# A two-layer gated cross-attention kernel: in the first network's second step, the first inner row's maximum and rounding are put behind the gate of the step's second block

## The chip, the cores and the metric

The kernel runs on one core of a Trainium2 chip. The metric is device time in microseconds (us) of one execution. Three timed executions of the kernel before gave 729.78, 729.82 and 726.80 us; the median is 729.78 us. One more execution was recorded by the hardware profiler.

## The reference, cut to what matters

The input x has 8 x 256 = 2048 rows of 512 values. Four stages change it one after the other, each added to x with a gate factor tanh(g):

1. a long convolution of the context with 32 heads, multiplied with the normalised x,
2. a first feed-forward network with weights rounded to -1, 0 or 1 and activations rounded to 8 bits,
3. a masked attention over the context,
4. a second feed-forward network with signs for weights.

The change lies in stage 2. For each row of x:

```python
def _activation_quant(x):
    scale = 127.0 / jnp.clip(jnp.max(jnp.abs(x), axis=-1, keepdims=True), 1e-05, None)
    xq = jnp.clip(jnp.round(x * scale), -128.0, 127.0) / scale
...
h = jax.nn.silu(_bitlinear(x, w1)) * _bitlinear(x, w2)      # 512 -> 1408
return _bitlinear(h, w3)                                    # 1408 -> 512
```

`_bitlinear` first rounds its input row by row. So the inner row h, 1408 values wide, needs its absolute maximum over the whole row before it can be scaled, rounded to int8 and sent through the third weight.

## The kernel before, in words

The 2048 rows are cut into 16 tiles of 128 rows, one row for each partition. Stage 2 is a loop of 17 steps (`for t in range(NT + 1)`), software-pipelined by hand: the order of the statements is the order in which each engine gets its instructions, since the program is under a manual schedule. Each engine works through its own list in that order; waits between engines are semaphores which the tile framework puts in. In step t the kernel

- makes the inner row of tile t, `hh` (128 x 1408), in three blocks of columns, by `up_block` (L854 to L872) at columns 0, 512 and 1024. This document calls them blocks A, B and C; A and B are 512 wide, C is 384 wide. A block is four matmuls on TensorE into `pa` and four into `pb` (L860), a SiLU of `pa` on ScalarE into `sl` (L868), and the gate on VectorE, `hh = pb * f * sl` (L869). `pa` and `pb` come from a ring of four PSUM buffers, so that the `pa` of a block takes the buffer of the `pa` two blocks earlier and waits for that block's SiLU, and its `pb` waits for that block's gate. Block A of step 2 waits in this way for block B of step 1;
- takes the maximum of the inner row of tile t-1 on VectorE by `row_max(h_[t - 1], "h")` (the maximum at L518, then two small instructions at L520 and L522 that end in the scale `sc`), and rounds this row on ScalarE into `i8h` (L1019), GpSimd clips it to bf16 into `qh` (L1037), and a transposing DMA on the SyncE queue brings it to the layout that TensorE needs, `hqT` (L1039);
- multiplies the inner row of tile t-2 by the third weight on TensorE (`down0`, L877, eleven matmuls into `po`); tile 0 is done at the end of step 2;
- prepares tile t+2: `front_norm` on ScalarE (L201), `front_max` on VectorE (L518 again, on 512 columns), `front_int` on ScalarE (L537), `front_turn` on GpSimd and the SyncE queue (L541 to L545), which ends in the transposed `xqT`;
- in steps 1 to 3 also finishes stage 1 for the tiles with odd numbers: `odd_back` transposes a tile back on TensorE (`tr_back`, L424), ScalarE scales it out of PSUM (`back`, L989), GpSimd adds it to x (L990). There are two PSUM buffers for these transposes, so that the third `tr_back`, the first of step 2, waits for the first `back`;
- in step 1 also makes the reciprocal deviations of four tiles by `ln_finish` (three small instructions on VectorE, then fourteen on GpSimd).

From step 2 on, the maximum of the previous inner row stands ahead of block A's gate, and its rounding ahead of block B's SiLU. In step 1 of the kernel before it is:

- VectorE: gate of block A, the three instructions of `ln_finish`, maximum of inner row 0, maximum of the front row 3, gate of block B, gate of block C;
- ScalarE: SiLU of block A, rounding of inner row 0, SiLU of block B, rounding of the front row 3 (`i8x`), `back`, SiLU of block C, `back`, normalisation of the front row 4, and then step 2's SiLU of block A.

The lines of before which the change touches are L1013 to L1019, between `up_block(*x0[t], hh, 0)` and `up_block(*x0[t], hh, 512)`:

```python
if t == 1:

    ln_finish(*FINISH[0])
    inv, sc = row_max(h_[0], "h")
if 1 <= t:
    q = p1.tile([P, FF0], I8, tag="i8h", name="i8h")
    nc.scalar.activation(q, h_.pop(t - 1), AF.Copy, scale=sc)
```

Of the kernel before, what the change touches and what calls it, by code (L numbers as in the profile page):

```python
# [12 lines left out]
I8 = mybir.dt.int8  # L13
# [3 lines left out]
AF = mybir.ActivationFunctionType  # L17
# [4 lines left out]
P = 128  # L22
# [11 lines left out]
FF0, FF1 = 1408, 2048  # L34
# [8 lines left out]
def flamingo_gated_kernel(  # L43
# [15 lines left out]
    nc = tc.nc  # L59

    def pool(stack, name, bufs, **kw):
        return stack.enter_context(tc.tile_pool(name=name, bufs=bufs, **kw))
# [146 lines left out]
    def load_table(func):  # L209

        nc.scalar.activation(junk1, ln_eps, func)
# [15 lines left out]
    def residual(t, po, factor):  # L227
        nc.vector.scalar_tensor_tensor(
            xs[:, t, :], po, factor, xs[:, t, :], op0=ALU.mult, op1=ALU.add
        )  # L230
# [284 lines left out]
    def row_max(v, tag):  # L515

        am = small.tile([P, 1], F32, tag="am" + tag, name="am")
        nc.vector.tensor_reduce(am, v, AX.X, ALU.max, apply_absolute_value=True)  # L518
        inv = small.tile([P, 1], F32, tag="inv" + tag, name="inv")
        nc.vector.tensor_scalar(inv, am, Q_EPS, 1.0 / 127.0, ALU.max, ALU.mult)  # L520
        sc = small.tile([P, 1], F32, tag="sc" + tag, name="sc")
        nc.vector.reciprocal(sc, inv)  # L522
        return inv, sc

    def front_norm(k):
        xn0[k] = pf.tile([P, L], F32, tag="xn", name="xn2")
        if k < GRP:
            ln_apply_act(xn0[k], order0[k], *firsts[k // 2], k % 2)
        else:
            ln_apply_act(xn0[k], order0[k], *st0[k // GRP][1:], k % GRP)  # L530
# [305 lines left out]
    p1 = pool(s_mid, "p2one", 1, side="right", reuse_waits="tile")  # L836
# [17 lines left out]
    def up_block(xqT, f1, hh, f0):  # L854
        fw = min(512, FF0 - f0)
        pa = ps_mm.tile([P, 512], F32, tag="mm", name="pa")
        pb = ps_mm.tile([P, 512], F32, tag="mm", name="pb")
        for i, pp in ((0, pa), (1, pb)):
            for c in range(NL):
                nc.tensor.matmul(  # L860
                    pp[:, :fw],
                    xqT[:, c, :],
                    w0q[i][:, c, f0 : f0 + fw],
                    start=(c == 0),
                    stop=(c == NL - 1),
                )
        sl = p2.tile([P, 512], F32, tag="sl", name="sl")
        nc.scalar.activation(sl[:, :fw], pa[:, :fw], AF.Silu, scale=f1[:, 0:1])  # L868
        nc.vector.scalar_tensor_tensor(  # L869
            hh[:, f0 : f0 + fw], pb[:, :fw], f1[:, 1:2], sl[:, :fw],  # L870
            op0=ALU.mult, op1=ALU.mult,
        )  # L872
# [11 lines left out]
    scale = 1.0 / math.sqrt(L)  # L884
# [34 lines left out]
    def batch_gate(neg):  # L919

        valid = small.tile([P, 1], F32, tag="valid", name="valid")
        nc.vector.tensor_reduce(valid, neg, AX.X, ALU.max)
        gv = small.tile([P, 1], F32, tag="gv", name="gv")
        nc.vector.tensor_scalar(gv, valid, 0.0, gate_x[1], ALU.is_equal, ALU.mult)
        return gv

    def normalised3(t, by_pool=False):
        xn = p3.tile([P, L], F32, tag="xn", name="xn3")
        rstd, nmr = st3[t // GRP][1:]
        if by_pool:  # L930
            c = slice(t % GRP, t % GRP + 1)
            nc.gpsimd.tensor_scalar(xn, xs[:, t, :], rstd[:, c], nmr[:, c], ALU.mult, ALU.add)
        else:
            ln_apply_act(xn, t, rstd, nmr, t % GRP)
        return xn
# [12 lines left out]
    def scores(xT, cT):  # L948
        ps = ps_mm.tile([P, 512], F32, tag="mm", name="ps")
        for c in range(NL):  # L950
            nc.tensor.matmul(  # L951
                ps[:, :S], xT[:, c, :], cT[:, c, :], start=(c == 0), stop=(c == NL - 1)
            )
        return ps
# [30 lines left out]
    def odd_back(t):  # L985

        back_transpose(t)
        o = pc.tile([P, L], F32, tag="xn", name="back")
        nc.scalar.activation(o, trs.pop(t), AF.Copy, scale=gate_x[0])  # L989
        return lambda: nc.gpsimd.tensor_tensor(xs[:, t, :], xs[:, t, :], o, ALU.add)  # L990

    h_, d_, hq_ = {}, {}, {}

    BACK = {1: [0, 1], 2: [2, 3, 4], 3: [5, 6, 7]}
    signs, sums, made = [], [], 0
    for t in range(NT + 1):
        new = t + 2 < NT
        if t < NT:
            hh = p2.tile([P, FF0], F32, tag="hh", name="hh")
        if new and t > 0:  # L1000
            front_norm(t + 2)
        if t > 1:
            inv, sc = row_max(h_[t - 1], "h")
        if t == NT:
            xn_[2] = normalised3(2)
            load_table(AF.Exp)
            gates3 = {0: batch_gate(negs[0])}
            ps_ = {k: scores(xT_.pop(k), keys[0]) for k in range(2)}
        if t < NT:
            up_block(*x0[t], hh, 0)  # L1010
        if t == 0:
            front_norm(t + 2)
        if t == 1:  # L1013

            ln_finish(*FINISH[0])
            inv, sc = row_max(h_[0], "h")
        if 1 <= t:
            q = p1.tile([P, FF0], I8, tag="i8h", name="i8h")
            nc.scalar.activation(q, h_.pop(t - 1), AF.Copy, scale=sc)  # L1019
        if t == NT - 2:  # L1020
            xn_ = {k: normalised3(k) for k in range(2)}
        if t >= 3:
            residual(order0[t - 3], *d_.pop(t - 3))
        back = BACK.get(t, [])
        if len(back) == 3:
            sums.append(odd_back(odds[back[0]]))
        if new:
            front_max(t + 2)
        if t < NT:
            up_block(*x0[t], hh, 512)  # L1030
        if t == NT - 1:
            xT_ = {k: x_transposed(xn_.pop(k), True) for k in range(2)}
        if new:
            front_int(t + 2)
        if 1 <= t:
            b = p2.tile([P, FF0], BF16, tag="qh", name="qh0")
            nc.gpsimd.tensor_scalar(b, q, 127.0, -128.0, ALU.min, ALU.max)  # L1037
            bT = p_hq.tile([P, NF0, P], BF16, tag="hqT", name="hqT")
            nc.sync.dma_start_transpose(out=bT, in_=b)  # L1039
            f3 = small.tile([P, 1], F32, tag="f3", name="f3")  # L1040
            nc.gpsimd.tensor_scalar(f3, inv, gw0, None, ALU.mult)
            hq_[t - 1] = (bT, f3)
        if t == NT - 2:
            keys, values = {0: load_keys(0)}, {0: load_values(0)}
        if new:
            front_turn(t + 2)
        for add in sums:
            add()
        sums = []
        if back:  # L1050
            sums.append(odd_back(odds[back[-2]]))
        if t > 2:
            hqT, f3 = hq_.pop(t - 2)
            d_[t - 2] = (down0(hqT), f3)
        if t in FINISH and t > 0:
            ln_finish(*FINISH[t])

        for k in STATS3.get(t, ()):
            ln_moments_of(st3, natural, k, "3")
        if t > 0:  # L1060
            for k in STATS0.get(t, ()):
                ln_moments_of(st0, order0, k, "0")
        if t < NT:
            up_block(*x0.pop(t), hh, 1024)
            h_[t] = hh
        if t == 2:

            hqT, f3 = hq_.pop(0)
            d_[0] = (down0(hqT), f3)
        if back:  # L1070
            sums.append(odd_back(odds[back[-1]]))
        for add in sums:
            add()
        sums = []
        if t == 0:
            clip_by_act(2, 3)
        if t == 3:
            s_conv.close()
            wp1 = pool(ctx, "w1", 1, reuse_waits="tile")
            w1q = [wp1.tile([P, NL, FF1], F32R, name=f"w1_{i + 1}") for i in range(2)]  # L1080
            p_st = pool(s_att, "w1st", 3, reuse_waits="tile")
        if t == NT - 3:
            p3 = pool(s_att, "p3", 2, reuse_waits="tile")
        if t < NT:
            for make in signs:
                make()
            signs = []
        if 3 <= t < NT:
            signs = [w1_signs(made + k) for k in range(2)]
            made += 2  # L1090
        if t == NT - 2:
            bytes_ = {b: load_mask(b) for b in range(2)}
        if t == NT - 1:
            negs = {0: key_mask(bytes_.pop(0))}
        if t == NT:
            negs[1] = key_mask(bytes_.pop(1))
# [105 lines left out]
    for t in range(NT + 2):  # L1202
# [19 lines left out]
        if t == NT:  # L1222
            xn4, q, back = front(1)
# [60 lines left out]
        if t == NT - 3:  # L1284
            q = front_int4(xn4, back)
# [15 lines left out]
    with ExitStack() as ph:  # L1301
# [11 lines left out]
        p1 = pool(ph, "p4one", 1, reuse_waits="tile")  # L1313
# [186 lines left out]
```

## Time and profile before

| | before |
|---|---|
| median of 3 timed executions | 729.78 us (726.80 to 729.82) |
| the profiled execution: its time | 731.69 us |
| the profiled execution: span from first to last instruction | 729.8 us |
| TensorE busy | 713.4 us of the span |
| VectorE busy | 598.6 us |
| ScalarE busy | 371.6 us |
| GpSimd busy | 260.8 us |
| mean granted TensorE clock | 0.992 of full speed |

Engines in the profile are PE (TensorE's matmuls), PEld (its weight loads, which overlap the matmuls), DVE (VectorE), ACT (ScalarE), POOL (GpSimd) and SPq (the queue of SyncE that issues DMAs). A row of the timeline has the start in us from the span's start, the time in us, the engine, the line, the operation with output and input, and in brackets the idle time ahead of it with what ended it. Stage 1 fills the span's first 181 us, the loop of stage 2 goes from 181 us to about 315 us, and the two later stages take the rest. Step 1 of the loop begins at 185.9 us, step 2 at 194.7 us.

### The profile page before, as it was taken

The numbers are of one execution on the slowest core, as the hardware profiler recorded it, in microseconds if no ns is written. First come the engines' busy times: TensorE is split into PE (matmuls) and PEld (weight loads), VectorE is DVE, ScalarE is ACT, GpSimd is POOL, SyncE is SP. The second block draws the span as 40 slices with busy tenths as digits, with TensorE's granted clock in tenths as the row PEclk, the third lists the DMA queues.
The fourth block names the chain that finished last, engine by engine and source line by source line (L and its number), as shares of the span: only waits on it lengthen the run. The fifth ranks groups of instructions, "written<-read, shape, count | busy, mean of one in ns | idle before, by whom it ended". The sixth has DMA issues, their size and how long they took to land.

```text
span 729.8 us, 10128 instructions
## 1 busy us (share of the span) xinstructions
PE 713.4 (98%) x3200; PEld 532.0 (73%) x3200; DVE 598.6 (82%) x1224; ACT 371.6 (51%) x669; POOL 260.8 (36%) x366
## 2 busy tenths in 40 slices
PE   7999999999899999899999999999999999999997
PEld 6777777777454444556668888888888888888885
DVE  5799888999788888777868988988888988777965
ACT  5577887879777777657652222322222332212322
POOL 4788997989874535245300020000200002000000
PEclk8999999999999999999999999999999999999999
DMA  5775676831136565797704455544553444554443
GB/s 196 238 240 159 188 266 202 281 85 32 35 84 139 141 142 141 159 279 219 225 27 96 103 110 110 115 96 110 113 115 83 110 103 104 118 110 91 102 90 86
DMA packets 149970, 99.36 MB, mean 136 GB/s; under 512 B 83806, under 2 KB 127838, under 8 KB 149918
## 3 DMA queue, kind: packets, MB, share of 16 engines
q1 hardware_dynamic: 149608, 98.38, 51.2%
q0 software_dynamic: 256, 0.26, 1.0%
q8 instruction: 25, 0.41, 0.2%
q14 instruction: 27, 0.22, 0.1%
q10 hardware_dynamic: 54, 0.08, 0.1%
HBM read 75.58 MB, written 5.03 MB: 110 GB/s over the span
## 4 chain that ended last, share of the span: by engine, by line
PE 82%; DVE 5%; DMA 4%; POOL 3%; issue 3%; ACT 2%; SPq 0%; DVEq 0%; ACTq 0%; POOLq 0%
PE y L349 17%; PE po L1375 16%; PE pb L1181 15%; PE pa L1181 15%; PE po L877 4%; PE pa L860 4%; PE pb L860 4%; PE po L980 2%; PE ps L951 2%; DMA w1st<-in_L_w3t 2%; DMA hqT<-qh 1%; POOL kv L326 1%; PE tr L416 1%; POOL prod L394 1%; DMA sT<-d 1%
## 5 line engine op out<-in xcount | busy, mean ns | idle before, releaser
L349 PE MATMUL y<-kv,toep 128*128 128x288 f32 x640 | 161.1, 409 | 0.9 <-DVE prod L384 0.7
L349 PEld LDWEIGHTS y<-kv,toep 128*128 128x128 f32 x640 | 120.1, 191 | 33.5 <-ACT qx L313 0.9
L1189 ACT ACTIVATE sl<-pa,wmean 128x512 f32<-128x512 f32 x64 | 44.0, 688 | 195.1 <-PE pa L1181 195.1
L1375 PE MATMUL po<-w,lo 128*128 128x512 f32 x256 | 99.9, 390 | 0.0
L1375 PE MATMUL po<-w,hi 128*128 128x512 f32 x256 | 99.6, 389 | 0.0
L181 POOL TENSOR_TENSOR nwt<-rstd 128x4 f32<-128x4 f32 x33 | 6.6, 199 | 235.1 <-DVE rstd L176 233.2
L326 POOL TENSOR_TENSOR kv<-cx 128x1024 f32<-128x1024 f32 x32 | 60.6, 1895 | 24.2 <-ACT cx L313 24.0
L1181 PE MATMUL pa<-w,hi 128*128 128x512 f32 x256 | 69.2, 392 | 0.0
L1181 PE MATMUL pb<-w,hi 128*128 128x512 f32 x256 | 68.6, 390 | 0.1
L1181 PE MATMUL pa<-w,lo 128*128 128x512 f32 x256 | 68.5, 389 | 0.0
L1181 PE MATMUL pb<-w,lo 128*128 128x512 f32 x256 | 68.4, 389 | 0.0
L860 PEld LDWEIGHTS <-xqT 128*128 128x128 bf16 x384 | 37.9, 99 | 41.2 <-issue 3.1
L394 POOL TENSOR_TENSOR prod<-prod 128x1024 f32<-128x1024 f32 x28 | 66.3, 2368 | 0.0
L1155 ACT CAST hi<-v 128x512 fp32r<-128x512 f32 x64 | 39.2, 622 | 47.9 <-DVE v L1365 47.9
L1193 DVE SCALAR_TENSOR_TENSOR hh<-pb,wmean,sl 128x512 f32<-128x512 f32 x64 | 47.8, 747 | 14.7 <-PE pb L1181 14.5
L1375 PEld LDWEIGHTS po<-w,lo 128*128 128x128 f32 x256 | 48.0, 188 | 10.9 <-DVE lo L1160 1.0
L1181 PEld LDWEIGHTS pa<-w,hi 128*128 128x128 f32 x256 | 47.8, 188 | 10.8 <-ACT hi L1155 0.6
L1181 PEld LDWEIGHTS pb<-w,hi 128*128 128x128 f32 x256 | 48.0, 188 | 10.5 <-DVE hh L1193 0.6
L1181 PEld LDWEIGHTS pa<-w,lo 128*128 128x128 f32 x256 | 48.1, 188 | 10.0
L1375 PEld LDWEIGHTS po<-w,hi 128*128 128x128 f32 x256 | 48.1, 188 | 9.9
L1181 PEld LDWEIGHTS pb<-w,lo 128*128 128x128 f32 x256 | 48.0, 188 | 10.0
L371 DVE TENSOR_TENSOR prod<-y,qx 128x512 f32<-128x512 f32 x64 | 43.8, 684 | 8.6 <-ACT y L359 4.4
(163 smaller groups left out, 1345.3 us busy)
## 6 DMA issues: line engine op xcount, KB each, us to landing
sT<-d SPq DMA_DIRECT2D x64, 256.0 KB
toep<-ssm_skip SPq DMA_DIRECT2D x31, 256.0 KB
ch<-in_ctx_heads SPq DMA_DIRECT2D x32, 128.0 KB
w1a<-in_L_w1t SPq DMA_DIRECT2D x8, 512.0 KB
w1a<-in_L_w2t SPq DMA_DIRECT2D x8, 512.0 KB
w1st<-in_L_w1t SPq DMA_DIRECT2D x16, 256.0 KB
w1st<-in_L_w2t SPq DMA_DIRECT2D x16, 256.0 KB
cT<-in_ctx_t SPq DMA_DIRECT2D x8, 512.0 KB
```

What stands on the lines that cost most here:

```text
L326: nc.gpsimd.tensor_tensor(kv[:, :, 0 : ND * HD].rearrange("p a (i d) -> p a i d", d=ND), cx[:, :, 0:HD].unsqueeze(3).to_broadcast([P, NL * ...
L349: nc.tensor.matmul(y[:, k, :, W0 : W0 + NPAIR], toeps[h][:, d * P : (d + 1) * P], kvs[h][:, mi * B : (mi + 1) * B, :].rearrange("p b n -> ...
L371: nc.vector.tensor_tensor(prod[:, 0, r, :, :], yv[:, :, W0 : W0 + ND * HD].rearrange("p a (i d) -> p a i d", d=ND), view(q, [HX, n], [1, H ...
L394: nc.gpsimd.tensor_tensor(flat[0], flat[0], flat[1], ALU.add)
L860: nc.tensor.matmul(pp[:, :fw], xqT[:, c, :], w0q[i][:, c, f0 : f0 + fw], start=(c == 0), stop=(c == NL - 1),)
L877: nc.tensor.matmul(po, hqT[:, c, :], w0q[2][:, c, :], start=(c == 0), stop=(c == NF0 - 1))
L951: nc.tensor.matmul(ps[:, :S], xT[:, c, :], cT[:, c, :], start=(c == 0), stop=(c == NL - 1))
L1155: nc.scalar.copy(hi, v)
L1181: nc.tensor.matmul(pp, xT[k][:, c, :], w1q[i][:, c, f0 : f0 + 512], start=(c == 0 and k == 0), stop=(c == NL - 1 and k == 1),)
L1189: nc.scalar.activation(sl, pa, AF.Silu, scale=wmean1[:, 0:1])
L1193: nc.vector.scalar_tensor_tensor(hh, pb, wmean1[:, 1:2], sl, op0=ALU.mult, op1=ALU.mult)
L1375: nc.tensor.matmul(po, hT[b][k][:, c, :], w1q[2][:, b * NL + c, :], start=(b == 0 and c == 0 and k == 0), stop=(b == NB - 1 and c == NL - ...
```

## The change

It leaves `ln_finish` where it is, puts the rounding into a small function, and moves the maximum and the rounding of inner row 0 from ahead of block B to behind it in step 1 alone. All other steps issue what they issued before.

```diff
+    def hidden_int(k, sc):
+        q = p1.tile([P, FF0], I8, tag="i8h", name="i8h")
+        nc.scalar.activation(q, h_.pop(k), AF.Copy, scale=sc)
+        return q
...
         if t == 1:
-
             ln_finish(*FINISH[0])
-            inv, sc = row_max(h_[0], "h")
-        if 1 <= t:
-            q = p1.tile([P, FF0], I8, tag="i8h", name="i8h")
-            nc.scalar.activation(q, h_.pop(t - 1), AF.Copy, scale=sc)
+        if t > 1:
+            q = hidden_int(t - 1, sc)
...
         if t < NT:
             up_block(*x0[t], hh, 512)
+        if t == 1:
+
+            inv, sc = row_max(h_[0], "h")
+            q = hidden_int(0, sc)
```

The order of instructions in step 1 becomes:

- VectorE: gate of block A, the three of `ln_finish`, maximum of the front row 3, gate of block B, maximum of inner row 0, gate of block C;
- ScalarE: SiLU of block A, SiLU of block B, rounding of inner row 0, rounding of the front row 3, `back`, SiLU of block C, and so on as before.

The lists of TensorE, GpSimd and the SyncE queue keep their order. No instruction is added or taken away.

## The prediction

> **What bounds the kernel now.** I read the page first. TensorE is busy for 98% of the span, so only TensorE's idle time, or its slow time, can be won. Then I asked who TensorE's matmuls waited for between 186 and 203 us, around the change:
>
> ```profile
> PE 713.4 (98%) x3200; PEld 532.0 (73%) x3200; DVE 598.6 (82%) x1224; ACT 371.6 (51%) x669; POOL 260.8 (36%) x366
> ```
> ```profile
> PE pa L860 <- ACT sl L868: 3.0, 1, 3.0
> ```
>
> One wait of 3.0 us, and it is the place that the change touches. The chain of work that ended last, followed through 186 to 203 us, leaves TensorE just here (start, us, what):
>
> ```profile
> 189.35 0.75 DVE hh L869
> ...
> 190.69 1.53 DVE am L518
> ...
> 192.60 0.59 DVE am L518
> ...
> 194.01 0.68 ACT sl L868
> ...
> 194.73 1.16 PE pa L860 x4
> ```
>
> The gate of block 1A, the maximum of inner row 0, then the SiLU of block 1B, which frees the PSUM buffer that `pa` of block 2A takes. The timelines of ScalarE, TensorE and its weight loads show why:
>
> ```profile
> 188.64 0.67 ACT L868 ACTIVATE sl<-pa,f 128x512 f32<-128x512 f32 x1
> 192.64 1.47 ACT L1019 ACTIVATE i8h<-hh,sc 128x1408 int8<-128x1408 f32 x1 [3.32 <-DVE sc L522]
> 194.01 0.67 ACT L868 ACTIVATE sl<-pa,f 128x512 f32<-128x512 f32 x1
> 194.58 0.71 ACT L537 ACTIVATE i8x<-xn,sc 128x512 int8<-128x512 f32 x1
> 195.19 0.67 ACT L989 ACTIVATE back<-tr_back,gates 128x512 f32<-128x512 f32 x1
> 195.76 0.57 ACT L868 ACTIVATE sl<-pa,f 128x384 f32<-128x384 f32 x1
> ```
> ```profile
> 191.08 0.60 PE L424 MATMUL tr_back<-ident,qT 128*128 128x128 f32 x4
> 194.73 1.16 PE L860 MATMUL pa<-w,xqT 128*128 128x512 bf16 x4 [3.05 <-ACT sl L868]
> 195.68 1.91 PE L860 MATMUL pb<-w,xqT 128*128 128x512 bf16 x4
> 197.39 1.06 PE L424 MATMUL tr_back<-ident,qT 128*128 128x128 f32 x4
> 198.24 1.36 PE L860 MATMUL pa<-w,xqT 128*128 128x512 bf16 x4
> ```
> ```profile
> 192.75 0.10 PEld L860 LDWEIGHTS <-xqT 128*128 128x128 bf16 x1 [1.31 <-DMA xqT<-qx]
> ```
>
> ScalarE stands for 3.32 us at the rounding of inner row 0, with the ready SiLU of 1B behind it, and TensorE stands for 3.05 us. Two more things are to be seen. The weight load shows that block 2A could not have begun before 192.75 us: its transposed input came then. And behind the stall four groups take from 194.73 to 199.43 us, 4.70 us, where groups of these sizes take 0.86 + 0.86 + 0.43 + 0.87 = 3.02 us at full clock: 1.68 us more. The table of windows says why (busy us of PE, PEld, DVE, ACT and POOL, then the granted clock):
>
> ```profile
> 192.00:195.40 3.40, 0.67 (x4) 0.41 (x5) 2.12 (x7) 2.76 (x4) 2.58 (x11) 1.00 0.04 8
> 195.40:198.90 3.50, 3.50 (x12) 1.85 (x11) 2.49 (x5) 2.79 (x5) 3.23 (x6) 0.51 0.49 93
> ```
>
> The clock was halved for 3.4 us behind the stretch in which TensorE did 0.67 us of work. So the place costs 3.05 + 1.68 = 4.73 us, of which 1.2 us (191.68 to 192.85, the weight load included) is the input's and stays. From 202 to 277 us TensorE is busy without a gap and the clock is 1.00: what is won or lost at the first third-weight product (`po`, at 202.03 us) is passed on whole.
>
> **The change, step by step.** Times are those of the profiled execution; an engine's instructions follow each other by their start-to-start distances in its rows.
>
> VectorE. The third instruction of `ln_finish` starts at 190.52, the next at 190.60. In place of inner row 0's maximum the front row's comes first. Its three instructions take 0.97 us (192.52 to about 193.49 in before). Then the gate of 1B at 191.57: its SiLU is long done, and it takes 0.66 us to the next start, 0.75 alone (ends 192.32). Then inner row 0's maximum, 192.23, with 2.04 us from its start to the rounding's start on ScalarE, as before (190.60 to 192.64). So the rounding starts at 194.27, not 192.64: 0.97 + 0.66 = 1.63 us later.
>
> ScalarE. The SiLU of 1B is ahead of the rounding now: 188.64 + 0.57 = 189.21, ended by 189.9 (its matmuls ended at 188.65). This takes 0.57 us out from behind the rounding. All that is queued behind it (the front row's rounding, `back`, SiLU of 1C, `back`, normalisation, SiLU of 2A) is therefore 1.63 - 0.57 = 1.06 us later than before: `i8x` at 195.64, the first `back` at 196.25 (ends 196.92), SiLU of 1C at 196.82 (ends 197.39), SiLU of 2A at 198.56 (ends 199.23).
>
> TensorE. `pa` of 2A starts at 192.85, as soon as its input is there, and not at 194.73. `pb` at 193.71 (the gate of 1B ended at 192.32), ended 194.57. Next in its list is the third `tr_back`, which needs the PSUM buffer of the first: `back` ends at 196.92, so it starts at 197.07. This is a new stall of 2.50 us, in place of the old one of 3.05. Then `pa` of 2B at 197.50 (SiLU of 1C ended 197.39), `pb` at 198.36 (gate of 1C: 197.43 to 198.05), `tr_back` at 199.22, `pa` of 2C at 199.65. `pb` of 2C needs the gate of 2A. On VectorE this stands behind the gate of 1C and the maximum of inner row 1, all 1.06 us later than before: 198.98 + 1.06 = 200.04, ended 200.79. So `pb` of 2C at 200.83, and `po` at 201.48, against 202.03: 0.55 us earlier, if the clock stays full.
>
> What else is moved. The rounded row 0 is ready at 195.74; GpSimd's clip goes from 194.76 to 195.78, the transposing DMA behind it on SyncE's queue from 196.15 to 197.17, and the front row's DMA behind that from 197.71 to 198.73, with GpSimd's additions. The nearest row for the landing, the last such transpose, is 3.50 us from issue (308.75) to TensorE's start (312.25): 200.67, 0.81 us ahead of `po`. The front row's is wanted at 204.3. Both are at no cost; the cover is TensorE's own work up to 201.48, and without it each us of delay is a us. The next inner row's rounding (200.13, not 199.13) and its transpose (issued 203.03, so landed by about 206.5) are wanted at 208.6. No queue is blocked that TensorE reads from later.
>
> **The unknown: the clock behind the new stall.** In the place of one gap of 3.05 us there are two, 1.2 and 2.50 us, with 1.72 us of matmuls between. The Trainium skill, "TensorE: Matmul & The Clock Gate", section "Why this matters for your kernels", asks for no gaps over about 3 us between bursts; by that rule the new gaps leave the clock alone and the sum is -0.55. The page's Part 1 has free-running windows of 3413 ns, which fits the 3.4 us here. The rows speak for a stricter gate. The clock falls after a window with 0.67 us of work in 3.40. At the start of the span it falls too, and stays low, with far more:
>
> ```profile
> 4.33:7.74 3.41, 2.15 (x17) 1.74 (x15) 2.78 (x10) 1.52 (x3) 2.09 (x2) 1.00 0.96 342
> 7.74:11.15 3.41, 2.12 (x9) 1.73 (x10) 3.24 (x13) 2.93 (x6) 0.99 (x2) 0.50 0.70 261
> ```
>
> 63% busy by matmul spans was not enough. The emptiest window I found that kept the clock, 308.1 to 311.5 us, has 2.53 us, 74%. With the boundary of before (195.4) the new windows hold 1.72 us (50%) and 1.8 us (53%); with any other, one holds less, down to 0.91 us (27%). So I expect one cold window. Its cost depends on its place: from 195.4 to 198.9 it slows `tr_back` and most of `pa` 2B, but the wait for the gate of 2A takes some of it back, and `po` comes at 201.86, 0.17 us earlier than before. From 198.0 to 201.4 it slows 2B's `pb` and `tr_back`, and `po` comes at 202.5, 0.5 later; the worst single place I find is 0.6 later. Ends: -0.55 (no cold window) and +1.5 (two, below); below -0.55 is excluded, as the chain over VectorE to the gate of 2A does not run on TensorE's clock. I take +0.2, the middle of one cold window's -0.2 to +0.6: 731.69 + 0.2 = 731.9 us for a profiled execution. The median of the runs lies 1.91 us under the profiled execution (729.78 to 731.69), so 730.0 us.
>
> **The rivals.**
>
> - *The stall moves and the clock stays full.* -0.55: 729.2 us. For it speaks the skill's 3 us, against it the start of the span. Chance 0.25.
> - *The stall is gone.* All but the input's 1.2 us is won: 4.73 - 1.17 = 3.56 us, 726.2 us. It needs ScalarE to come to `back` in time; but the rounding cannot start before 194.27, and `back` and the SiLU of 1C are behind it. Chance 0.04.
> - *Slower: the clock stays low for two windows.* Place: 195.4 to 202.3 us. It decides if the window from 195.4 to 198.9, 53% busy at half clock, is too empty to raise the clock again; at the span's start one with 62% was. Then `pa` 2B ends at 199.63, `pb` 201.34, `tr_back` 202.19, 2C at about 203.55, and `po` is 1.5 us later than before: 731.3 us. Chance 0.18.
> - *The transposed row 0 is late.* At 299.02 a transpose took 5.36 us beside weight loads; from 197.17 that ends at 202.53, +0.5: 730.3 us. Between 196 and 200 us the queue moves only these two transposes, so it is unlikely: 0.05.
>
> **How the numbers follow.** Forecast 0.48, at 730.0 (729.6 to 730.4 by itself). The executions of one and the same kernel are 726.80 to 729.82, a spread of 3.0 us whose cause no row shows and which is larger than all cases but one. So the range is 726.8 (the lowest run; a little above the case of no stall) to 732.0 (two cold windows and half a window's loss more). 0.5% is 3.65 us, about what a measurement of this kernel can tell from no change: under 726.1 is faster, over 733.4 slower. Only the vanished stall comes near the first, only two cold windows together with an unlucky spread near the second: 0.05 and 0.05, same 0.90.
>
> **What would show it.** In the changed kernel's timelines: the SiLU of 1B near 189.2 and the rounding near 194.3 with about 4.4 us idle ahead of it; TensorE's 3.05 us wait replaced by two, the second of about 2.5 us at a `tr_back` that waits for `back`; the third-weight product between 201.5 and 203.6; in the table of windows the clock at 0.5 for one stretch between 193 and 202. It is wrong if the rounding starts before 194, if the second gap is missing, or if the times differ by more than 2 us in either direction with the loop's later steps no longer contiguous.

## The result, and the profile after

The changed kernel takes 729.37 us (median of 12 executions, 727.5 to 732.8), the kernel before 729.80 us (12 executions, 726.8 to 732.12). The ratio of after to before on record is 1.0006 with a 95% interval of 0.9991 to 1.0021; the quotient of the two medians, 0.9994, lies inside it. A second comparison gave 1.0012 (0.9998 to 1.0027). No difference that can be measured.

The profiled execution of after took 732.8 us, the longest of the twelve; its span is 731.0 us, and TensorE is busy for 715.5 us of it. The rows below answer to those shown of before. First the waits of TensorE between 186 and 206 us:

```profile
PE tr_back L424 <- ACT back L989: 2.3, 1, 2.3
PE pa L860 <- DMA xqT<-qx: 1.3, 1, 1.3
```

One wait of 3.0 us has become two, of 1.3 and 2.3 us, with other names: `pa` of block 2A waits for its input, and the third transpose waits for `back`. The timelines of ScalarE and TensorE:

```profile
189.16 1.25 ACT L868 ACTIVATE sl<-pa,f 128x512 f32<-128x512 f32 x2
194.85 1.47 ACT L996 ACTIVATE i8h<-hh,sc 128x1408 int8<-128x1408 f32 x1 [4.44 <-DVE sc L522]
...
196.84 0.67 ACT L989 ACTIVATE back<-tr_back,gates 128x512 f32<-128x512 f32 x1
197.41 0.57 ACT L868 ACTIVATE sl<-pa,f 128x384 f32<-128x384 f32 x1
```
```profile
193.33 1.04 PE L860 MATMUL pa<-w,xqT 128*128 128x512 bf16 x4 [1.25 <-DMA xqT<-qx]
...
197.56 0.66 PE L424 MATMUL tr_back<-ident,qT 128*128 128x128 f32 x4 [2.33 <-ACT back L989]
198.05 1.45 PE L860 MATMUL pa<-w,xqT 128*128 128x512 bf16 x4
199.29 1.91 PE L860 MATMUL pb<-w,xqT 128*128 128x512 bf16 x4
...
203.19 2.54 PE L877 MATMUL po<-w,hqT 128*128 128x512 bf16 x11
```

The two SiLUs (x2) now run one behind the other at 189.16, but the rounding begins only at 194.85, and `back` and the SiLU of 1C behind it. `pa` and `pb` of block 2B are slow again. The windows (busy us of PE, PEld, DVE, ACT, POOL, then the clock):

```profile
195.10:198.50 3.40, 1.07 (x8) 0.70 (x8) 0.49 (x1) 3.40 (x6) 2.05 (x4) 1.00 0.00 0
198.50:201.90 3.40, 3.40 (x12) 1.77 (x11) 3.30 (x6) 2.47 (x4) 3.11 (x4) 0.50 0.76 145
```

The clock is halved for one window of 3.4 us here too, about 3 us later in the span than in before.

Step 1 starts at slightly different times in each execution, so from here on places are counted from the start of block 1A's gate on VectorE (189.35 us in before, 189.87 in after). The **measure** is the time from there to the first matmul of the first third-weight product: 202.03 - 189.35 = 12.68 us in before, 203.19 - 189.87 = 13.32 us in after.

### The profile page after: what moved, and what is told of

The parts are those of the page before. It is cut to its first block, busy times and chain, and to the rows that moved or that the text cites. A ratio compares the mean times of both kernels' runs of the same rounds, so it can differ in the third digit from the quotient of the medians.

```text
span 731.0 us, 10128 instructions
## 1 busy us (share of the span) xinstructions
PE 715.5 (98%) x3200; PEld 534.2 (73%) x3200; DVE 598.6 (82%) x1224; ACT 371.5 (51%) x669; POOL 260.3 (36%) x366
## 4 chain that ended last, share of the span: by engine, by line
PE 89%; DMA 4%; DVE 3%; issue 2%; POOL 1%; ACT 1%; SPq 0%; DVEq 0%; ACTq 0%; POOLq 0%
PE y L349 22%; PE po L1382 16%; PE pb L1188 15%; PE pa L1188 15%; PE po L877 4%; PE pa L860 4%; PE pb L860 4%; PE po L980 3%; PE ps L951 3%; DMA hqT<-qh 1%; PE tr L416 1%; PE tr_back L424 1%; DMA w1st<-in_L_w3t 1%; PE tr L940 1%; DMA sT<-d 1%
```

## The experiments

The theory is the prediction's: the change takes away the wait for the SiLU of 1B, but makes the rounding 1.63 us later on VectorE, and what stands behind the rounding on ScalarE 1.06 us later; so TensorE stalls again, and the clock can fall behind either stall. The rivals: another bound holds the stretch anyway (the transposed input, GpSimd); or the clock is no part of it.

| kernel | measure, us | stretch at half clock in it | ratio to before, 95% interval |
|---|---|---|---|
| before; once more | 12.68; 12.70 | yes; yes | |
| after; once more | 13.32; 12.15 | yes; no | 1.0006 (0.9991 to 1.0021); 1.0012 (0.9998 to 1.0027) |
| before, gap filled | 11.10 | no | 0.9971 (0.9957 to 0.9985) |
| after, gap filled | 12.15 | no | 0.9986 (0.9966 to 1.0005) |
| ScalarE's half alone | 10.52 | no | 0.9976 (0.9961 to 0.9991) |
| after, `back` ahead of the rounding | 11.58 | no | 0.9996 (0.9983 to 1.0009) |
| after, inner row ahead of front row | 11.20 | no | 0.9995 (0.9981 to 1.0009) |

One microsecond is 0.14%, about the half-width of these intervals; so the measure of the profiled executions carries the argument, and the ratios only say whether it is contradicted.

**ScalarE's half alone.** The maximum stays where it was, the rounding is moved:

```diff
         if t == 1:
             ln_finish(*FINISH[0])
+            inv, sc = row_max(h_[0], "h")
...
         if t == 1:
-
-            inv, sc = row_max(h_[0], "h")
             q = hidden_int(0, sc)
```

> One half of the change alone: on ScalarE the rounding of inner row 0 stands behind the SiLU of block 1B, on VectorE its maximum stays ahead of the gate of 1B. The measure is the time from the gate of block 1A (VectorE) to the first third-weight product (TensorE): 12.68 us before, 13.32 us after. Theory: the old stall comes from ScalarE's order alone, and what spoils the change is VectorE's half, which makes the rounding 1.63 us later. Then here the rounding starts as early as before (3.3 us behind the gate of 1A, not 5.0), everything behind it on ScalarE is 0.6 us earlier than before, TensorE's gaps are the input's 1.2 us and several of under 0.6 us, the clock is not halved, and the measure is 10.6 us: about 2.1 us less time than before, 0.3%. Rival (the transposed input or the transposed inner row is the bound): the measure stays at 12.0 us or more and the time is within 0.7 us of before.

Measured: 12.68 becomes 10.52 us, and the time is 0.9976 of before (0.9961 to 0.9991), about 1.8 us less. ScalarE and TensorE in this kernel, whose gate of 1A is at 187.67 us:

```profile
190.97 1.47 ACT L996 ACTIVATE i8h<-hh,sc 128x1408 int8<-128x1408 f32 x1 [2.75 <-DVE sc L522]
...
192.96 0.67 ACT L989 ACTIVATE back<-tr_back,gates 128x512 f32<-128x512 f32 x1
```
```profile
191.09 1.04 PE L860 MATMUL pa<-w,xqT 128*128 128x512 bf16 x4 [1.09 <-DMA xqT<-qx]
192.63 1.02 PE L860 MATMUL pb<-w,xqT 128*128 128x512 bf16 x4 [0.50 <-DVE hh L869]
193.68 0.65 PE L424 MATMUL tr_back<-ident,qT 128*128 128x128 f32 x4
```

The rounding stands 3.3 us behind the gate of 1A, as in before, and `back` frees the transpose's buffer just as TensorE comes to it. The stall of before was ScalarE's order alone; VectorE's half is what spoils the change. Its interval lies below 1, so it is faster than before, and it only touches those of after (0.9991 to 1.0021, and 0.9998 to 1.0027) at its upper end: this half of the change beats both kernels (after by way of before; the two were not timed side by side). VectorE's half alone was not tried: with the rounding still ahead of the SiLU of 1B and its maximum behind the gate of 1B, each of the two engines would wait for the other for ever.

**Each stall by its name.** In after, the first `back` is issued ahead of the rounding:

```diff
         if t == 1:
-
+            sums.append(odd_back(odds[back[-2]]))
             inv, sc = row_max(h_[0], "h")
             q = hidden_int(0, sc)
...
-        if back:
+        if back and t > 1:
             sums.append(odd_back(odds[back[-2]]))
```

> The changed kernel, with the first scaling of a transposed tile out of PSUM (back) issued ahead of the rounding of inner row 0 on ScalarE. Theory: the new stall at the third transpose is this back's place in ScalarE's list. Here that transpose follows block 2A at once, and the wait goes on to the next thing behind the rounding, the SiLU of 1C, for which block 2B waits about 1.9 us. Measure from the gate of 1A to the first third-weight product: 11.6 us at full clock, up to 12.4 with a cold window (after: 13.32). Rival (the third transpose waits for something else, for instance for GpSimd's addition): the gap ahead of the transpose stays over 2 us and the measure stays at 13 us.

The measure is 11.58. TensorE's rows:

```profile
191.86 0.60 PE L424 MATMUL tr_back<-ident,qT 128*128 128x128 f32 x4
194.24 1.02 PE L860 MATMUL pa<-w,xqT 128*128 128x512 bf16 x4 [1.78 <-ACT sl L868]
```

The transpose no longer waits; the wait goes to the next thing behind the rounding, the SiLU of 1C. The third transpose was held by nothing else.

**What VectorE puts ahead of the rounding.** In after, the front row's maximum goes behind inner row 0's:

```diff
-        if new:
+        if new and t != 1:
             front_max(t + 2)
...
             inv, sc = row_max(h_[0], "h")
             q = hidden_int(0, sc)
+            front_max(t + 2)
```

> The changed kernel, with the maximum of the front row 3 behind that of inner row 0 on VectorE. It takes one of the two things away (0.97 of the 1.63 us) that the change put ahead of the rounding on VectorE. Theory: the rounding starts 4.0 us behind the gate of 1A (after: 4.98), all that stands behind it on ScalarE is as much earlier, the wait of the third transpose shrinks from 2.3 to 1.4 us, and the measure from the gate of 1A to the first third-weight product is 11.2 us at full clock (after: 13.32 with a cold window, 12.15 with its gap filled). Rival (the front row's rounding, now waiting for its maximum, holds ScalarE instead): the transpose's gap stays over 2 us and the measure at 12.1 us or more.

The rounding stands 193.43 - 189.44 = 3.99 us behind the gate of 1A (4.98 in after), the wait ahead of the transpose is 1.35 us, the measure 11.20:

```profile
196.14 0.66 PE L424 MATMUL tr_back<-ident,qT 128*128 128x128 f32 x4 [1.35 <-ACT back L989]
```

So of the 1.69 us by which after starts the rounding later than before (4.98 against 3.29), the front row's maximum is 0.99, and the other 0.70 stay with the gate of 1B still ahead. The ratio, 0.9995 (0.9981 to 1.0009), shows no gain: the profiled execution's 1.5 us less than before would be 0.9980, just outside the interval. That execution kept its clock; an estimate further down suggests that some of the timed ones did not.

**The clock.** The stalls are filled with matmuls whose result is not used; all other instructions and their order stay:

```diff
+        if t == 2:
+            fill = ps_o.tile([P, L], F32, tag="o", name="fill")
+            for _ in range(9):
+                nc.tensor.matmul(fill, w0q[0][:, 0, :P], w0q[0][:, 0, :L], start=True, stop=True)
```

in after behind `up_block(*x0[t], hh, 0)`, and in before the same with twelve matmuls ahead of it.

> The changed kernel with nine extra matmuls of 128x512 (about 1.9 us, their result is not used) put into TensorE's new gap between block 2A and the third transpose. Theory of the clock: the halved clock behind the gap costs the changed kernel about 1.2 us, and a gap that is filled leaves the clock at 1.00; the measure from the gate of 1A to the first third-weight product falls from 13.32 to about 12.1 us and the time by about 1.2 us. Rival (the clock falls anyway, or its loss is hidden by the waits for VectorE): the measure stays at 13.0 us or more.

> The kernel before with twelve extra matmuls of 128x512 (about 2.6 us, their result is not used) put into TensorE's old gap of 3.05 us ahead of block 2A. Theory: with the clock kept at 1.00 the kernel before reaches the first third-weight product 1.6 us earlier: measure from the gate of 1A 11.1 us, not 12.68, and then the order of before is a whole 1.0 us better than the changed order with its gap filled: the change by itself makes the path longer, and only the clock's loss, which comes in both, hides it. Rival (the clock makes no difference to the end of this stretch): measure 12.6 us, and the two filled kernels equal.

Measured: 12.15 and 11.10 us. TensorE in before with its gap filled (gate of 1A at 186.93):

```profile
189.10 2.75 PE L1012 MATMUL fill<-w 128*128 128x512 bf16 x12
192.34 1.02 PE L860 MATMUL pa<-w,xqT 128*128 128x512 bf16 x4 [0.48 <-ACT sl L868]
193.20 1.03 PE L860 MATMUL pb<-w,xqT 128*128 128x512 bf16 x4
194.06 0.60 PE L424 MATMUL tr_back<-ident,qT 128*128 128x128 f32 x4
```

`pa` of 2A still waits for the same SiLU and starts no earlier (192.34 - 186.93 = 5.41 us behind the gate of 1A, 194.73 - 189.35 = 5.38 in before), but what follows takes 1.03 and 0.60 us, not 1.91 and 1.06. So before's stall costs 12.68 - 11.10 = 1.6 us by the clock alone. And with the clock held, the changed order is 12.15 - 11.10 = 1.05 us longer than the order of before. The change has a loss of its own, the 1.06 us forecast on ScalarE; what hides it is that before pays for a cold clock more often than after does, as the executions below show.

After and before once more, for the clock:

> The changed kernel once more, for its clock. Theory: its stall is the same to 0.1 us in each execution (2.3 us at the third transpose, 1.25 us at block 2A), and whether the clock is halved behind it depends on how the clock's windows fall: measure from the gate of 1A to the first third-weight product 12.1 us without a cold window, up to 13.4 us with one. Rival: the measure is 13.3 us again with the clock at 1.00, and the clock is no part of it.

> The kernel before once more, for its clock. Theory: stall of 3.05 us again, measure from the gate of 1A to the first third-weight product 11.1 us without a cold window, 12.7 us or a little more with one. Rival: 12.7 us with the clock at 1.00.

After again (gate of 1A at 187.76): the same two waits, no cold window, measure 12.15.

```profile
191.19 1.04 PE L860 MATMUL pa<-w,xqT 128*128 128x512 bf16 x4 [1.10 <-DMA xqT<-qx]
195.41 0.65 PE L424 MATMUL tr_back<-ident,qT 128*128 128x128 f32 x4 [2.32 <-ACT back L989]
195.90 1.03 PE L860 MATMUL pa<-w,xqT 128*128 128x512 bf16 x4
```

Before again: 3.06 us of stall, half clock from 196.1 to 199.5 us, measure 12.70. In each profile the recorded changes of the clock lie whole steps of 3.413 us apart (in before, those at 7.75, 195.48 and 727.96 us are 55.0 and 156.0 steps from one another), so the windows can be placed also where nothing changes. Those of both, after first (cut at steps of 3.4 us back from where its clock falls at the end of the span), then before:

```profile
190.10:193.50 3.40, 1.90 (x8) 0.70 (x8) 2.50 (x4) 0.80 (x1) 2.17 (x11) 1.00 0.15 28
193.50:196.90 3.40, 1.49 (x9) 0.97 (x10) 1.00 (x2) 3.40 (x6) 2.38 (x4) 1.00 0.01 3
```
```profile
192.70:196.10 3.40, 1.07 (x5) 0.58 (x6) 1.82 (x6) 3.17 (x5) 2.68 (x9) 1.00 0.00 0
196.10:199.50 3.40, 3.40 (x12) 1.75 (x11) 2.73 (x5) 2.47 (x6) 3.13 (x6) 0.50 0.61 115
```

In after's second profile the idle time was split over two windows, which kept 56% and 44% of work and the full clock. In before's second profile 1.07 us (31%) were left in one, and the clock fell. In after's first profile it was 1.07 us too.

How often this happens can be estimated from the mean granted clock, which is on record for the timed executions too. In the ten profiles it is 0.999 or 1.0 without a cold window, 0.998 with one at this place, 0.994 to 0.995 with two near the span's start, and 0.992 to 0.993 with both. Sorted by this (0.997 put with 0.998, 0.996 with 0.995), 77 of 117 executions of before had a cold window here, 11 of 34 of after, 2 of 21 of before with its gap filled, and 6 of 22 of the kernel with the inner row first. With the measures above that makes 11.10 + 0.66 x 1.6 = 12.2 us for before and 12.15 + 0.32 x 1.2 = 12.5 us for after, a difference of about 0.4 us or 0.05%, which both intervals of after allow.

**A version that removes all of it.** The maximum of inner row 0 was kept early, everything that frees a buffer of TensorE was put ahead of the rounding, and the first third-weight product behind block 3A (edits cut to their core):

```diff
         if t == 1:
             ln_finish(*FINISH[0])
+            inv, sc = row_max(h_[0], "h")
...
         if t == 1:
+            sums.append(odd_back(odds[back[-2]]))
+            up_block(*x0.pop(t), hh, 1024)
+            h_[t] = hh
+            sums.append(odd_back(odds[back[-1]]))
             q = hidden_int(0, sc)
+            front_max(t + 2)
...
+        if t == 1:
+            front_turn(t + 2)
         if 1 <= t:
             b = p2.tile([P, FF0], BF16, tag="qh", name="qh0")
...
+        if t == 3:
+            hqT, f3 = hq_.pop(0)
+            d_[0] = (down0(hqT), f3)
```

> The order that the four earlier kernels point to, the maximum of inner row 0 kept early: VectorE: maximum of inner row 0, gates of 1B and 1C, then the front row's maximum; ScalarE: SiLU of 1B, back, SiLU of 1C, back, then the rounding of inner row 0 and the front row's; GpSimd: the front row ahead of inner row 0; the first third-weight product goes from the end of step 2 to behind block 3A. Measure here from the gate of 1A to the first matmul of block 3B, since the product has moved: 17.66 us before, 18.30 after, 15.49 in the kernel with ScalarE's half alone. Theory: TensorE keeps only the 1.2 us wait for its input and short waits of under 0.5 us, clock 1.00, measure 14.4 us, 3.2 us less time than before (0.44%). Rival (GpSimd's chain to the transposed rows is the bound in any order): the measure stays at 15.3 us or more, no better than ScalarE's half alone.

Measured from the gate of 1A (190.46) to block 3B (206.75): 16.29 us, worse than ScalarE's half alone (15.49); ratio to before 0.9990 (0.9971 to 1.0009). The theory missed by 1.9 us, and the rival's bound on the measure held. ScalarE and TensorE:

```profile
199.28 1.47 ACT L996 ACTIVATE i8h<-hh,sc 128x1408 int8<-128x1408 f32 x1 [1.26 <-POOL qh L1053]
200.90 0.69 ACT L989 ACTIVATE back<-tr_back,gates 128x512 f32<-128x512 f32 x1 [0.15 <-POOL xs L990]
```
```profile
201.64 0.66 PE L424 MATMUL tr_back<-ident,qT 128*128 128x128 f32 x4 [1.92 <-ACT back L989]
```

With the front row ahead on GpSimd, its clip of inner row 0 (`qh`) ends at 199.25; the next rounding writes the only `i8h` buffer and must wait for that, and the following `back` needs a buffer that GpSimd's additions free. So GpSimd holds this wait, as the rival had it, but by the buffers that it gives back and not by a late transposed row: I had reckoned only with its outputs.

## Why the prediction was right

729.37 us against 730.0, and "no measurable change": both held, and most steps can be checked against the two profiles of after. Times from the gate of 1A:

| step | predicted | after | after again |
|---|---|---|---|
| rounding of inner row 0 starts | 4.92 | 4.98 | 4.94 |
| first `back` starts | 6.90 | 6.97 | 6.93 |
| SiLU of 1C starts | 7.47 | 7.54 | 7.50 |
| third transpose starts | 7.72 | 7.69 | 7.65 |
| gate of 2A starts | 10.69 | 10.74 | 10.70 |
| third-weight product, full clock | 12.13 | | 12.15 |
| the same, one cold window | 12.5 to 13.3 | 13.32 | |

- *The stall of 3.05 us goes, 1.2 us of it stays as the wait for the input, and a new one of 2.50 us comes at the third transpose.* Shown: 1.25 and 2.33 us, and once more (1.10 and 2.32). The 0.17 us too many come from ending `pb` of 2A by its distance to the next start (0.86 us), where its row takes 1.03 us. The row of PEld with the input's wait had been visible under the larger stall all the time.
- *Everything behind the rounding on ScalarE is 1.06 us later.* Shown: counted from the gate of 1A, the first `back` is 1.13 us later than in before (6.97 against 5.84), and with the clock held in both, the changed order loses 1.05 us.
- *The transposed inner row is in time.* In no profile of after does the product wait for it.
- *The clock behind the new stall: "So I expect one cold window".* Right for the profiled execution, whose cold window lies where the prediction had put its dearer case (from 198.0 us in before's times): it had 0.5 us for it, and 0.64 us was measured. Its ground was only half right. I read the stretch from 4.33 to 7.74 us as a window of 63% work that had not been enough, and so held windows of 50% and 53% for cold. After's second profile kept the clock with a window of 44%. The 63% are time in the rows of matmuls, and the short rows of that stretch say too much: counted by columns (an estimate: 0.108 us for 128 f32 columns and 0.216 us for 512 bf16 columns, from the 0.43 and 0.86 us that four such matmuls take from start to start), it holds about 35%. So whether the clock falls depends on the execution, and by the estimate above it fell in only a third of the executions of after. That the +0.2 us taken for one cold window in each is near the mean was luck within its bounds: the prediction also held before's cold window for constant. The two profiles of after give +0.64 and -0.53 us against before's 12.68, and the timed runs cannot tell one from the other.
- *Slower: the clock stays low for two windows* did not occur at this place in any of the profiles; but neither did its premise, a stretch of 53% work at half clock, so it stays open.
- *The stall is gone* was rightly held to be impossible for this order; the half change that leaves the maximum early comes 2.2 us (12.68 - 10.52) into the 3.56 us.
- *A spread of 3.0 us whose cause no row shows.* It is now partly explained, below.

## What to carry to other kernels

An engine that works in order passes a wait on to everything queued behind it; when an instruction is moved, look at what it waits for as well as at what waits for it. Moving the waiting instruction behind the urgent one (ScalarE's half) gained 2.2 us; moving its producer behind too (VectorE's half) cost 1.6 us at full clock (12.15 - 10.52) and 2.8 us with a cold window (13.32 - 10.52), because the producer's delay is added to everything else in the queue. Before a stall is removed, find the next limit under it: here the input's landing, the next buffer release, and the engine that frees the buffers were each 1 to 2.3 us behind.

## What the runs showed of the hardware that I had not expected

The granted clock fell behind gaps of 2.33 us as well as of 3.05, where the Trainium skill, "TensorE: Matmul & The Clock Gate", section "Why this matters for your kernels", warns of about 3 us. In the windows of 3.4 us around these gaps, what counted was the work left in one window: 31% or less and the next ran at half speed, 44% or more and it did not. The end of before's span puts the lower figure higher: the window from 724.55 to 727.96 us has 1.35 us of matmuls in 3.41 (40%), and the clock is 0.50 behind it.

In the first 20 us the time in rows does not sort the windows: 52% to 66% were followed by half speed in four of the ten profiles, and 46% to 77% by full speed in three others. Counted by columns, as above, the windows at full clock of all ten profiles are sorted by the estimate: at 37% or less the clock fell, at 42% or more it stayed, and between them both occur. Where windows fall differs from execution to execution, so that the same stall cost 0 or 1.2 us in after.

A large part of the scatter between profiled executions comes from the first 20 us, but not all. The gate of 1A starts between 186.70 us (the kernel with `back` first) and 190.46 us (the last version), with instructions that are the same in all kernels up to there; the time from the first third-weight product to the end of the span differs too, from 525.9 to 528.7 us in the nine other than the last version, and the cause of that is open. Transposes in the warm-up of these two, the faster first:

```profile
11.00 1.09 PE L416 MATMUL tr<-ident,xnp 128*128 128x128 f32 x8 [1.62 <-POOL xnp L705]
```
```profile
12.42 1.97 PE L416 MATMUL tr<-ident,xnp 128*128 128x128 f32 x8 [2.08 <-POOL xnp L705]
```

Eight transposes take 1.09 us in the one and 1.97 in the other, where the table of windows has the clock at 0.50, and start 1.4 us apart. In after they took 1.97 us too, where the table has 1.00; but the trace of after has no record of the clock before 17.6 us. So near the start of a span a 1.00 in the table can stand for no record, and the durations are to be read.
